# Pairwise products of 32 fields: VectorE keeps the order of the text

## The chip, the cores and the metric

The kernel runs on one core of a Trainium2 chip. The metric is the device time of one execution in microseconds (us), lower is better. The cited time is the median of three runs.

## The reference

The input is `r_x`, 4096 samples of 32 fields of 64 numbers each, and a 64 x 64 matrix `W`, all in 32-bit floats. Every field is multiplied by `W`, and then every pair of fields i < j gives one product, element by element:

```python
vid = jnp.einsum('bfd,de->bfe', x, W)
idx_i, idx_j = jnp.triu_indices(F_, k=1)      # F_ = 32: 496 pairs
return x[:, idx_i, :] * vid[:, idx_j, :]      # 4096 x 496 x 64
```

The input has 33.6 MB and the output 520 MB.

## The kernel before, in words

**Layout.** The host turns the samples so that the 64 numbers of a field lie across 64 partitions; two halves of the batch fill the 128 partitions. 128 samples of each half make one tile: 16 tiles, each 32 fields wide. One field (or one product) of a tile is a *unit* of 128 elements per partition. In SBUF there is one large buffer, `mem`, of 445 units, which holds everything: input tiles at the units in `XPLACE`, and products.

**Per tile** (loop of line 165), TensorE computes `vid` = x W for the 32 fields into PSUM, in eight blocks of four fields (two matmuls each, line 172). Then VectorE multiplies (line 196): one operand from `mem` (fields i), one from `vid` (fields j), the product into `mem`. `by_block` lists a tile's 496 pairs in blocks, and `products` cuts the blocks into instructions of 128 to 14336 elements per partition, 345 in all. Their order in the text is the order in which the products lie in the output.

**Slots.** The whole row of 16 x 496 products is cut into 70 runs, `SLOTS` (numbered from 0 here). Each names its length in units, the unit of `mem` where it is put, and the places ("seams") at which instructions are cut. When a slot's last product is written, line 199 issues one store of the whole slot to HBM. Slots overlap in `mem`: a later product writes where an earlier slot lay, and must wait until the parts that it overwrites have been stored. There are no pools that rotate; the list alone decides which store a product waits for. The slots that matter below:

| slot | units of `mem` | made by |
|---|---|---|
| 44, 45, 46 | 176 to 296, 297 to 413, 160 to 252 | tile 10 |
| 60 | 333 to 445 | tile 13 |
| 61 | 158 to 285 | tile 13 |
| 62 | 285 to 412 | end of tile 13, tile 14 |
| 63 | 64 to 191 | tile 14 |
| 64 | 192 to 319 | tile 14 |

Slots 65 to 69 follow to the end of tile 15.

**Order.** All transfers, loads and stores, are issued on the sync engine's queue (SP), in the order of the text. The kernel asks for that by name in line 121. For an engine that isn't named there, the framework's planner puts its instructions in an order of its own: it estimates when each can start and may let one pass others, as long as dependencies hold. Waits on semaphores are put in afterwards, for the order that results. VectorE isn't named in the kernel before, so its products may pass each other. Two of the 345 do:

- In tile 10, the 512-wide product of slot 46 (fields 0 to 3 with j = 24) stands ahead of four products that the text has before it: 8192 (the end of slot 44), 14336 and 512 (slot 45) and 1536 (the start of slot 46).
- In tile 14, the 10240-wide product of slot 63 (fields 0 to 15 with j = 16 to 20) stands ahead of five: 2048, 2048, 7168 and 768 (the end of slot 62) and 256 (the start of slot 63).

Of the kernel before, what the change touches and what calls it, by code (L numbers as in the profile page):

```python
# [52 lines left out]
def by_block():  # L53


    def within(lo):
        yield "step", lo, 2, 1, 0
        for k in range(2):
            yield "step", lo, 4, 2, k
        for i in (lo, lo + 8):  # L60
            yield "row", i + 4, i, 4, 4
        yield "row", lo + 8, lo, 8, 8

    yield from within(0)
    yield "row", 16, 0, 16, 16
    yield from within(16)


def products(blocks, at=0):

    for kind, a, b, c, d in blocks:
        if kind == "row":
            rows, n, i0, di, j0, dj = c, d, b, 0, a, 1
        else:
            rows, n, i0, di, j0, dj = 16 // b, c, a, b, a + c + d, b
        r = k = 0
        while r < rows:
            room = BREAKS[bisect_right(BREAKS, at)] - at
            if k or room < n:
                m, w = 1, min(n - k, room)  # L80
            else:
                m, w = min(rows - r, room // n), n
            yield at, m, w, i0 + r * di + k, di, j0 + r * dj, dj
            at += m * w
            if k + w == n:
                r, k = r + m, 0
            else:
                k += w
# [10 lines left out]
@with_exitstack  # L99
def pairwise_bilinear_kernel(  # L100
    ctx: ExitStack,
    tc: tile.TileContext,
    x0: bass.AP,
    x: bass.AP,
    out: bass.AP,
):

    nc = tc.nc
    NT = sum(len(tiles) for group in GROUPS for tiles in group)
    F = x0.shape[1] - 1 - PAD0
    D = P // 2
    NP = F * (F - 1) // 2

    BANK = 512 // C


    ctx.enter_context(tc.manual_schedule(engines={mybir.EngineType.SP}))

    const = ctx.enter_context(tc.tile_pool(name="const", bufs=1))
    psum = ctx.enter_context(
        tc.tile_pool(name="ps", bufs=1, space=bass.MemoryType.PSUM)
    )
    vid = psum.tile([P, F, C], F32)

    mem = const.tile([P, UNITS, C], F32)


    w2 = const.tile([P, D], F32)


    place = XPLACE[0]
    nc.sync.dma_start(  # L136
        out=mem.rearrange("p u c -> p (u c)")[:, place * C - D : (place + F // 2) * C],
        in_=x0.rearrange("p u c -> p (u c)")[:, C - D : (1 + F // 2) * C],
    )
    nc.sync.dma_start(out=mem[:, place + F // 2 : place + F, :], in_=x0[:, 1 + F // 2 : 1 + F, :])  # L140
    nc.vector.tensor_copy(w2, mem[:, place - 1, C - D :])  # L141
    loaded = 1

    def load(tiles, cuts=()):
        nonlocal loaded
        n = len(tiles) * F
        place = XPLACE[tiles[0]]
        at = (loaded - 1) * F
        loaded += len(tiles)
        return [  # L150
            nc.sync.dma_start(out=mem[:, place + lo : place + hi, :], in_=x[:, at + lo : at + hi, :])  # L151
            for lo, hi in cuts or [(0, n)]
        ]

    ready = mybir.DependencyInfo(mybir.DependencyClass.Sync, mybir.DependencyReason.DATA)

    def behind(later, earlier):
        tc.add_manual_dep(later.ins, earlier.ins.name, ready, reason="issued when that has landed")

    pieces = []  # L160
    groups, cuts = iter(GROUPS), iter(CUTS)
    for tiles, parts in zip(next(groups)[1:], next(cuts)):
        pieces = load(tiles, parts)

    for t in range(NT):
        xt = mem[:, XPLACE[t] : XPLACE[t] + F, :]


        for b in range(0, F, BANK):
            for h in range(2):  # L170
                half = slice(h * D, (h + 1) * D)
                nc.tensor.matmul(  # L172
                    vid[half, b : b + BANK, :],
                    lhsT=w2[half, :],
                    rhs=xt[half, b : b + BANK, :],
                    start=True,
                    stop=True,
                )

        for at, m, w, i, di, j, dj in products(by_block(), t * NP):  # L180
            slot = bisect_right(STARTS, at) - 1
            n = m * w
            begin, end = STARTS[slot], STARTS[slot + 1]
            ot = mem[:, SLOTS[slot][1] : SLOTS[slot][1] + SLOTS[slot][0], :]
            o = ot[:, at - begin : at - begin + n, :]
            if m == 1:
                left = xt[:, i : i + w, :]
                right = vid[:, j : j + 1, :].to_broadcast([P, w, C])
            else:
                o = o.rearrange("p (m w) c -> p m w c", m=m)  # L190
                right = vid[:, j : j + (m - 1) * dj + 1 : dj, :].unsqueeze(2).to_broadcast([P, m, w, C])
                if di == 0:
                    left = xt[:, i : i + w, :].unsqueeze(1).to_broadcast([P, m, w, C])
                else:
                    left = xt.rearrange("p (m d) c -> p m d c", d=di)[:, i // di : i // di + m, i % di : i % di + w, :]
            nc.vector.tensor_tensor(o, left, right, ALU.mult)  # L196
            at += n
            if at == end:
                store = nc.sync.dma_start(out=out[:, begin:end, :], in_=ot)  # L199
                if pieces:  # L200
                    behind(store, pieces[-2])
                    pieces.clear()


        if t + 2 == loaded < NT:
            (tiles,) = next(groups)
            pieces = load(tiles, next(cuts))
# [45 lines left out]
```

## Time and profile before

| | |
|---|---|
| time, median of 3 runs | 1291.11 us (1290.90 to 1291.38) |
| time of the profiled execution | 1290.48 us |
| span of the profiled execution, first to last instruction | 1288.7 us |
| VectorE busy (DVE) | 1084.0 us, 84% of the span, 346 instructions |
| TensorE busy (PE) | 219.6 us, 17%, 512 matmuls |
| transfers | 553.78 MB, 430 GB/s over the span |
| share of the 16 DMA engines taken by queue q1 | 99.6% |

The page has busy shares of the whole span and of 40 equal slices (32.2 us each), in tenths. "Idle before" in a row of a group is the time in which the engine had nothing running ahead of that instruction, with what ended it: `<-DMA out_dram<-mem` is the landing of an output transfer. A transfer is given from its issue to its landing, so it includes the time it waits behind others in the queue. The chain of waits goes back from the last instruction to what released it at each step.

### The profile page before, as it was taken

The page shows a single profiled execution, that of the slowest core. Times are in us where ns is not written, and L with a number is a line of the kernel's source. Part 1 is how long each engine was busy: PE and PEld are TensorE (multiplying, and loading weights), DVE is VectorE, ACT ScalarE, POOL GpSimd, SP SyncE. Part 2 cuts the span into 40 slices and gives each one's busy share as a digit, 9 for nine tenths or more (in the row PEclk, how much of TensorE's full clock was granted, in tenths as well). Part 3 has the DMA queues.
Part 4 walks back from the last instruction along what each step waited for, and adds up shares of the span by engine and source line. Part 5 has one row for each costly group of instructions (what it writes and reads, how often), then busy time and mean ns, then how long its engine had stood idle before and what let it go on. Part 6 is the DMA issues. An engine that isn't in the chain of part 4 may idle for free.

```text
span 1288.7 us, 1651 instructions
## 1 busy us (share of the span) xinstructions
PE 219.6 (17%) x512; PEld 42.2 (3%) x512; DVE 1084.0 (84%) x346; POOL 0.2 (0%) x4
## 2 busy tenths in 40 slices
PE   4031221203120213040312111103031130312000
PEld 1000000000000000000000000000000000000000
DVE  6899988899967389899799992859999889999942
POOL 0000000000000000000000000000000000000000
PEclk8555555656555556565555655555555565555555
DMA  9999999999999999999999999999999999989999
GB/s 416 432 423 439 443 436 423 434 424 443 420 453 411 422 435 431 443 439 430 423 442 427 433 443 430 423 418 432 447 433 418 441 440 418 448 361 452 435 414 412
DMA packets 11672, 553.78 MB, mean 430 GB/s; under 512 B 1296, under 2 KB 1296, under 8 KB 1680
## 3 DMA queue, kind: packets, MB, share of 16 engines
q1 hardware_dynamic: 11664, 553.69, 99.6%
q8 instruction: 4, 0.07, 0.0%
q14 instruction: 4, 0.03, 0.0%
HBM read 33.59 MB, written 520.09 MB: 430 GB/s over the span
## 4 chain that ended last, share of the span: by engine, by line
DMA 50%; DVE 42%; issue 6%; DVEq 0%; SPq 0%
DMA out_dram<-mem 45%; DVE mem L196 42%; DMA mem<-in_r_x_dram 5%; DVEq L241 0%; SPq L151 0%; DVEq L196 0%; SPq L140 0%; SPq L136 0%; SPq L199 0%
## 5 line engine op out<-in xcount | busy, mean ns | idle before, releaser
L196 DVE TENSOR_TENSOR mem<-mem,vid 128x1024 f32<-128x1024 f32 (+16 forms) x345 | 1083.8, 3213 | 173.6 <-DMA out_dram<-mem 168.1
L172 PE MATMUL vid<-mem,w 64*64 64x512 f32 x512 | 219.6, 988 | 961.1 <-DVE mem L196 853.3
L172 PEld LDWEIGHTS vid<-mem,w 64*64 64x64 f32 x512 | 42.2, 198 | 1137.3 <-DVE mem L196 984.8
L141 DVE COPY w<-mem 128x64 f32<-128x64 f32 x1 | 0.2, 195 | 5.8 <-DMA mem<-in_r_x_dram 5.8
L221 POOL MEMSET const-bfloat16-1.0<- 128x1 bf16 x1 | 0.1, 102 | 0.0
L221 POOL MEMSET const-uint8-127<- 128x1 uint8 x1 | 0.1, 102 | 0.0
L221 POOL MEMSET const-float32-0.0<- 128x1 f32 x1 | 0.1, 98 | 0.2 <-issue 0.2
L221 POOL MEMSET const-float32-1.0<- 128x1 f32 x1 | 0.1, 98 | 0.0
## 6 DMA issues: line engine op xcount, KB each, us to landing
out_dram<-mem SPq DMA_DIRECT2D x15, 8128.0 KB, 28.3
out_dram<-mem SPq DMA_DIRECT2D x14, 7680.0 KB, 24.6
out_dram<-mem SPq DMA_DIRECT2D x6, 7168.0 KB, 26.2
out_dram<-mem SPq DMA_DIRECT2D x5, 7936.0 KB, 28.1
out_dram<-mem SPq DMA_DIRECT2D x3, 7424.0 KB, 22.6
out_dram<-mem SPq DMA_DIRECT2D x3, 5888.0 KB, 20.9
mem<-in_r_x_dram SPq DMA_DIRECT2D x2, 8128.0 KB, 38.7
out_dram<-mem SPq DMA_DIRECT2D x2, 8064.0 KB, 24.4
```

The lines of the kernel that those rows point to most:

```text
L141: nc.vector.tensor_copy(w2, mem[:, place - 1, C - D :])
L172: nc.tensor.matmul(vid[half, b : b + BANK, :], lhsT=w2[half, :], rhs=xt[half, b : b + BANK, :], start=True, stop=True,)
L196: nc.vector.tensor_tensor(o, left, right, ALU.mult)
L221: nc = _bacc.Bacc("TRN2", target_bir_lowering=False, num_devices=1, dynamic_dma_scratch_size=1024)
```

## The change

VectorE is named beside the sync engine in the call that keeps the order of the text. Nothing else is edited.

```diff
-    ctx.enter_context(tc.manual_schedule(engines={mybir.EngineType.SP}))
+    ctx.enter_context(tc.manual_schedule(engines={mybir.EngineType.SP, mybir.EngineType.DVE}))
```

The built programs differ in this way: the two products above stand at their places in the text, and semaphore counts and waits follow that. In tile 14 the wait for slot 60's store, which the first 2048-wide product of slot 62's end had behind the 10240-wide one, now stands ahead of that product with nothing between. The instructions of TensorE, SP and GpSimd have the order they had.

## The prediction

> **What bounds the kernel now.** First the page's rows by 40 slices and its table of queues: they tell which resource is full, and where it isn't.
>
> ```profile
> DVE  6899988899967389899799992859999889999942
> ...
> DMA  9999999999999999999999999999999999989999
> GB/s 416 432 423 439 443 436 423 434 424 443 420 453 411 422 435 431 443 439 430 423 442 427 433 443 430 423 418 432 447 433 418 441 440 418 448 361 452 435 414 412
> ...
> q1 hardware_dynamic: 11664, 553.69, 99.6%
> ```
>
> The one hardware queue keeps the 16 DMA engines busy for 99.6% of the span, while VectorE (DVE) has slices at 2 and 3 tenths. The transfers are the bound. One slice alone shows an 8 in the DMA row and 361 GB/s: the 36th, 1128 to 1160 us. The table of stretches counts packets by their start and fixes the place:
>
> ```profile
> 1128.00:1131.00 3.00, 0.00 (x0) 0.00 (x0) 3.00 (x1) 0.00 (x0) 0.50 0.80 347
> 1131.30:1135.80 4.50, 1.65 (x4) 0.47 (x6) 4.50 (x4) 0.00 (x0) 0.50 0.00 0
> 1136.00:1139.00 3.00, 1.82 (x6) 0.14 (x2) 3.00 (x3) 0.00 (x0) 0.50 0.80 347
> ```
>
> The last two columns are DMA share and GB/s (with packets of 2.1 us counted by their start, 0.80 is what a full 3 us stretch shows here). From 1131.3 to 1135.8 us no packet starts at all, while VectorE is busy for the whole 4.50 us. It is the only such stretch: the queue has run dry. The chain of waits says what it waited for:
>
> ```profile
> 1061.31 0.06 DVE mem L196
> ...
> 1096.97 11.13 DVE mem L196 x6
> 1108.10 0.99 issue
> 1109.09 25.89 DVE mem L196 x8
> 1134.98 20.59 DMA out_dram<-mem
> ```
>
> The transfer issued at 1134.98 is slot 62's store. Ahead of it stand 73.7 us of products from 1061.31, with no wait between. The groups of VectorE between 1111.5 and 1134.9 us, shapes kept apart, show what ran last (busy us, mean ns, idle before):
>
> ```profile
> L196 DVE TENSOR_TENSOR mem<-mem,vid 128x10240 f32<-128x10240 f32 x1 | 10.8, 10809 | 0.0
> L196 DVE TENSOR_TENSOR mem<-mem,vid 128x7168 f32<-128x7168 f32 x1 | 7.6, 7611 | 0.0
> L196 DVE TENSOR_TENSOR mem<-mem,vid 128x2048 f32<-128x2048 f32 x2 | 4.5, 2276 | 0.0
> L196 DVE TENSOR_TENSOR mem<-mem,vid 128x768 f32<-128x768 f32 x1 | 0.9, 943 | 0.0
> ```
>
> The 10240-wide product belongs to slot 63; the four others finish slot 62. The planner put the former first.
>
> **What the Trainium skill says.** "Perfetto Trace Analysis", Optimization Strategy: look for gaps on the engine that bounds, and for what ends them; here that is the one hole above. "DMA: Bandwidth & Descriptors", Where 436 GB/s comes from, puts the ceiling of the SBUF ports at 435 GB/s, and about 358 for traffic with HBM; this trace runs at 430 with HBM, so it agrees with the first and not the second, and there is no rate left to gain. The same page, Why a DMA increments its semaphore by 16: each engine posts its own share when its data are down, so a transfer has landed with its slowest engine. The trace agrees: slot 61's store posted from 1132.02 to 1134.04 us. "Runtime: NRT & Kernel Launch", Instruction fetch mechanics: instructions are refilled in 16 KiB blocks by DMA, "mostly hidden". The trace has four such blocks; the last, at 1113.1 us, took 0.88 us of one DMA engine, which then stood about 2 us behind the others. That is not hidden where DMA is the bound.
>
> **The change part by part.** Instructions, slots, transfers and the order of SP and PE stay; the two built programs differ in the place of two products and in semaphore counts.
>
> Tile 10. A 512-wide product of slot 46 (0.68 us at 798.6) goes back behind the 8192, 14336, 512 and 1536 that the planner had let it pass. Where it leaves, VectorE waits anyway until 809.40 for a landing (10.14 us idle). Where it arrives, 835.3, the next product waits until 852.99, after 17.64 us of idle time. It is covered by 17 us, and the stores of slots 44 and 45 do not depend on it: 0 us. Without that cover it would be 0.68.
>
> Tile 14. The 10240 goes back behind two 2048s, 7168 and 768 of slot 62 and 256 of slot 63. That adds a wait: the first 2048 overlaps slot 60 by one unit (333), so slot 60's store must have landed. Its row is the sole issue near 1089.29 us:
>
> ```profile
> out_dram<-mem SPq DMA_DIRECT2D x1, 7168.0 KB, 25.9
> ```
>
> It lands at 1089.29 + 25.9 = 1115.2. Until now the 10.81 us product hid that; now VectorE stands from 1111.36 to 1115.2, **3.9 us of idle time**, with the four products and slot 62's store queued behind it. From the start of the first 2048 (1122.09) to the issue (1134.98) took 12.9 us, so the store goes out at 1115.2 + 12.9 = **1128.1 instead of 1135.0**. Its first packet followed the issue by 0.85 us: 1129.0. The earliest DMA engine falls idle at 1131.7. The hole closes, with 2.7 us to spare, although VectorE loses time.
>
> What is late next: VectorE's 3.9 us. The whole group, 10240 included, is done 3.9 us later, so slot 63's store goes from 1141.57 to 1145.4; the queue, then full of slot 62's 8128 KB (19.2 us, by the landings at 1155.57, 1174.81 and 1194.08), needs it at about 1131.7 + 19.2 = 1150.9. Slot 64: a wait of 1.46 us for slot 62's landing vanishes, 1160.44 + 3.9 - 1.5 = 1162.9 against 1170. Slots 65 to 68 shift by +2.4 us and less (other waits on landings vanish too) against spare times of 9 us and more. The last store, slot 69's, waits for slot 67's landing (1250.23 before, some 2.7 earlier after) and goes out near 1260.7 against a queue that is dry at 1264 at the earliest. No new hole.
>
> What the closed hole is worth. The slowest DMA engine landed slot 61's store at 1134.04; without a hole it would land slot 62's 19.24 later, 1153.28, instead of 1155.57: **2.29 us**. The mean engine was idle 3.8 us (each engine's gap in the packet records, 2.25 to 4.28). The hole also let all engines start level again (posts within 0.2 us of each other from there to the end); now the laggard keeps its lag. How much of it? After an earlier block, at 151.8, a lag of 2.14 (posts of the landing at 165.3) was 1.57 at 316.9, 152 us later, as long as what is left here. So I take 0.5 us back: 2.29 + 0.5 = **2.8 us**, with 2.3 (no recovery) and 3.8 (full) as ends. Which engine the block at 1113 meets is not mine to know: five of the 16 already lagged by 0.5 to 0.9 (posts of slot 61), and if it meets one of these, the gain is that much less, 1.9 to 2.3, and without recovery 1.4.
>
> Sum: 0 - 2.8. The profiled execution's own time, 1290.48 (span 1288.7 and 1.8 around it), becomes 1287.7. It stood 0.6 under the median of 1291.11, so the forecast for the median is 1288.4, -0.21%.
>
> **The rivals.** 0.2%, 2.6 us, is about what a measurement of this kernel can tell from no change.
>
> A. The hole closes, but a lagging engine eats most of it (the block meets a late engine, or no recovery): gain 1.4 to 2.5, 1288.6 to 1289.7, within 0.2%. For it: the lag of 2 us in the trace. Against: eleven engines of sixteen were level before the block, and earlier lags shrank.
>
> B. Nothing changes: the new wait takes the old one's place. That needs a landing of slot 60 near 1122, so that slot 62's store goes out near 1135 again; 1291.1. Against: the landing is set by a queue that is full, and the queue's end moves with it.
>
> C. Slower: the wait on slot 60's landing costs VectorE more than the passed-over 10240 did. It decides from a landing at 1122.1 on (1134.98 - 12.9), 6.9 us later than the trace's; each further us is one of DMA. A landing at 1125 gives 1294.0. For it: VectorE has no reserve of finished slots there, being the chain from 1061 on. Against: 18.9 us of queue lie between slot 60's landing and slot 61's, and only 13.7 between it and slot 62's first packet.
>
> D. The order of the text isn't what is built: excluded by the built programs, SP's order included.
>
> **How the numbers follow.** Main case with gain above 2.6 (up to 3.8): 0.51. A, and the main case under 2.6: 0.40, with B's 0.03 inside 0.2%: 0.43. C: 0.06. The likeliest time is 1288.4. From the full recovery (1287.3) to the late engine (1289.7) lie some 8 in 10; runs differ by 0.25 either way, and part of B is taken in at the top: 1287.0 to 1290.4.
>
> **What would show it.** In the changed profile: no stretch without packets around 1131 to 1136 and no slice at 361 GB/s; a VectorE wait of about 3.9 us for an output transfer ending near 1115.2; stores issued near 1128.1 and 1145.4; idle times before slots 64, 66 and 67 gone or shorter; the last landing spread over 1 us or more instead of 0.2. It is wrong if a new dry stretch appears behind slot 63, or if the 2048 starts after 1122, or if the span stays over 1287.5 with the hole gone (then the lag was mis-sized).

## The result, and the profile after

| | before | changed |
|---|---|---|
| time, median of 13 runs | 1291.01 us (1290.40 to 1291.38) | 1288.00 us (1287.81 to 1288.50) |
| ratio | | 0.9978, 95% interval 0.9970 to 0.9986 |
| profiled execution: time, span | 1290.48, 1288.7 us | 1287.95, 1286.2 us |
| share of the DMA engines taken by q1 | 99.6% | 99.8% |

The changed kernel is faster by 3.0 us, 0.22%. The rows of the page that showed the hole:

```profile
DVE  6899988899967389899799992849999889899952
...
DMA  9999999999999999999999999999999999999998
GB/s 415 417 440 440 440 416 447 420 442 425 435 432 437 421 424 430 434 440 431 424 443 423 435 444 438 417 426 436 438 430 422 443 437 425 441 429 423 436 444 383
...
q1 hardware_dynamic: 11664, 553.69, 99.8%
```

The 36th slice, 361 GB/s before, has 429. The only low slice is the last, and that one merely ends with the work. The same three stretches as before:

```profile
1128.00:1131.00 3.00, 2.68 (x8) 0.42 (x4) 3.00 (x3) 0.00 (x0) 0.63 0.95 412
1131.30:1135.80 4.50, 0.00 (x0) 0.00 (x0) 4.50 (x1) 0.00 (x0) 0.76 1.07 462
1136.00:1139.00 3.00, 0.00 (x0) 0.00 (x0) 3.00 (x1) 0.00 (x0) 0.50 0.85 368
```

In the middle one the share has gone from 0.00 to 1.07 (full, with packets counted by their start). VectorE is as busy as it was; it does the 10240-wide product there. The chain of waits up to that place:

```profile
1061.77 0.06 DVE mem L196
1061.83 12.81 issue
1074.64 15.09 DVE mem L196
1089.73 0.02 issue
1089.74 25.45 DMA out_dram<-mem
1115.20 0.03 issue
1115.23 0.02 DVEq L196
1115.25 0.04 issue
1115.29 0.20 DVE mem L196
```

A transfer now stands in a stretch that was products alone: slot 60's store, issued at 1089.74 and landed at 1115.20, releases the first 2048-wide product. VectorE's groups from there to slot 62's store, with the idle time before them in the last column:

```profile
L196 DVE TENSOR_TENSOR mem<-mem,vid 128x7168 f32<-128x7168 f32 x1 | 7.6, 7615 | 0.0
L196 DVE TENSOR_TENSOR mem<-mem,vid 128x2048 f32<-128x2048 f32 x2 | 4.5, 2284 | 3.4 <-DMA out_dram<-mem 3.4
L196 DVE TENSOR_TENSOR mem<-mem,vid 128x768 f32<-128x768 f32 x1 | 0.9, 947 | 0.0
```

The wait is 3.4 us long and new. The 10240-wide product no longer stands among them, and slot 62's store goes out at 1128.20 instead of 1134.98; its issue in the sync queue:

```profile
1128.20 0.33 SPq L199 DMA_DIRECT2D out_dram<-mem  x1
```

Over the whole span, VectorE's waits for output transfers are no longer than before (168.1 us in 37 waits then), though one was added:

```profile
DVE mem L196 <- DMA out_dram<-mem: 165.2, 34, 21.1
```

Four short waits behind that place (1.46, 0.20, 1.41 and 1.53 us before, between 1155 and 1231 us) are gone; from 1128.42 to 1234.28 us VectorE now runs 33 products with no wait between.

### The profile page after: what moved, and what is told of

The parts are those of the page before. It is cut to its first block, busy times and chain, and to the rows that moved or that the text cites. A ratio compares the mean times of both kernels' runs of the same rounds, so it can differ in the third digit from the quotient of the medians.

```text
span 1286.2 us, 1653 instructions
## 1 busy us (share of the span) xinstructions
PE 216.8 (17%) x512; PEld 41.5 (3%) x512; DVE 1083.7 (84%) x346; POOL 0.2 (0%) x4
## 3 DMA queue, kind: packets, MB, share of 16 engines
q1 hardware_dynamic: 11664, 553.69, 99.8%
## 4 chain that ended last, share of the span: by engine, by line
DMA 48%; DVE 44%; issue 6%; DVEq 0%; SPq 0%
DVE mem L196 44%; DMA out_dram<-mem 42%; DMA mem<-in_r_x_dram 5%; DVEq L241 0%; SPq L151 0%; DVEq L196 0%; SPq L140 0%; SPq L136 0%; SPq L199 0%
## 5 line engine op out<-in xcount | busy, mean ns | idle before, releaser
L196 DVE TENSOR_TENSOR mem<-mem,vid 128x1024 f32<-128x1024 f32 (+17 forms) x345 | 1083.5, 3213 | 171.2 <-DMA out_dram<-mem 165.2
L172 PE MATMUL vid<-mem,w 64*64 64x512 f32 x512 | 216.8, 975 | 966.8 <-DVE mem L196 858.8
```

The source lines that it names most:

```text
L172: nc.tensor.matmul(vid[half, b : b + BANK, :], lhsT=w2[half, :], rhs=xt[half, b : b + BANK, :], start=True, stop=True,)
```

## The experiments

**Theory.** The span is set by the DMA queue. The tile 14 move closes the queue's only hole, and that is the whole gain; its size is set by the slowest of the 16 DMA engines, which a 16 KiB block of instructions had put about 2 us behind. **Rivals:** the tile 10 move has a share; VectorE's work or wait is itself on the path; a hole costs the mean idle time of the engines; the lag has another cause.

All times below are medians, with the ratio to the kernel before on the same chip. Each of the 16 DMA engines posts to the semaphore of a transfer when its share is done. The *spread* of a landing is the time from the first of the 16 posts to the last, and an engine's *lag* is how far its post is behind the first. Posts and single packets stand in the traces' records, and in none of the views shown here.

| variant | time, us | ratio (95% interval) | slot 62's store issued at |
|---|---|---|---|
| kernel before (three chip sessions) | 1291.00, 1290.84, 1290.95 | | 1134.98 |
| tile 10 move alone | 1290.88 | 0.9999 (0.9991 to 1.0007) | 1135.52 |
| tile 14 move alone | 1288.09 | 0.9977 (0.9969 to 0.9986) | 1128.44 |
| slot 62 later by two products | 1288.81 | 0.9982 (0.9976 to 0.9989) | 1133.18 |
| slot 62 later by four | 1293.50 | 1.0019 (1.0012 to 1.0027) | 1138.13 |
| wait partly filled | 1287.99 | 0.9978 (0.9969 to 0.9986) | 1128.98 |
| short TensorE stream | 1286.98, again 1287.24 | 0.9972 (0.9961 to 0.9983), 0.9970 (0.9959 to 0.9982) | 1127.37, 1127.20 |
| the same with a late block | 1288.12 | 0.9977 (0.9969 to 0.9986) | 1128.34 |
| changed kernel again | 1288.04 | 0.9976 (0.9966 to 0.9985) | 1126.71 |

**1. Which of the two moves.** Each variant takes the text's order and puts one product back by hand to where the planner had it. First, the tile 10 move alone:

```diff
+        work = list(products(by_block(), t * NP))
+        if t == 14:
+            work.insert(3, work.pop(8))
+        for at, m, w, i, di, j, dj in work:
-        for at, m, w, i, di, j, dj in products(by_block(), t * NP):
```

> Text order everywhere but in tile 14, where the 10240-wide product is put ahead of slot 62's four last products by hand: only the tile 10 move is left. Theory (the hole before slot 62's store is the whole gain): time as before, 1291.0 within 0.4; slot 62's store issued near 1135 us; a stretch without packets from about 1131.5 to 1135.8. Rival (VectorE is the bound, and each product that passes others costs something): part of the 3.0 us remains, 1288.5 to 1290.

Measured: 1290.88, as the kernel before. The hole is back; the stretch table has

```profile
1131.30:1135.80 4.50, 1.12 (x4) 0.29 (x4) 4.50 (x4) 0.00 (x0) 0.50 0.04 14
```

a DMA share of 0.04. The tile 10 move is worth nothing. The counterpart is the same edit with `t == 10` and `work.insert(5, work.pop(9))`:

> Text order everywhere but in tile 10, where the 512-wide product of slot 46 passes four others as before: only the tile 14 move is left. Theory: the same as the changed kernel, 1288.0 within 0.4; slot 62's store issued near 1128.2. Rival (the tile 10 move has a share): 1288.7 to 1290.

Measured: 1288.09, the whole gain, with the stretch full:

```profile
1131.30:1135.80 4.50, 0.00 (x0) 0.00 (x0) 4.50 (x1) 0.00 (x0) 0.88 1.07 462
```

**2. How much a hole costs.** The changed kernel with slot 62's store made later by repeats of one of its products, here two:

```diff
-            nc.vector.tensor_tensor(o, left, right, ALU.mult)
+            for _ in range(3 if (t, m, w, i, j) == (14, 4, 4, 8, 12) else 1):
+                nc.vector.tensor_tensor(o, left, right, ALU.mult)
```

> The changed kernel with the second 2048-wide product of slot 62's end made three times instead of once (same values): VectorE gets 2 x 2.2 = 4.4 us more work, slot 62's store goes out at about 1132.6, its first packet starts at 1133.5. Theory (the end is set by the slowest DMA engine, which falls idle only at about 1133.9): most engines stand idle for 1 to 1.5 us and nothing is lost, 1288.0 to 1288.3, and the last landing's spread falls from 1.45 to 0.3 to 0.8. Rival (a hole costs its mean length over the engines): +1.0 to 1.3, 1289.0 to 1289.3. Rival (VectorE's work is the path): +4.4, 1292.4.

Measured: 1288.81, 0.8 above the changed kernel (spans 1286.9 and 1286.2). The store's issue in the sync queue, and a stretch of the hole:

```profile
1133.18 0.33 SPq L199 DMA_DIRECT2D out_dram<-mem  x1
```

```profile
1132.40:1133.90 1.50, 1.50 (x4) 0.42 (x6) 1.50 (x3) 0.00 (x0) 0.50 0.00 0
```

No packet of data starts for 1.5 us, and yet most of the gain stays. All three expectations were missed, the theory's too (its time, and a last spread of 0.3 to 0.8, where 0.22 was measured). The store was 0.6 us later than I had reckoned: a repeat takes 2.32 us rather than 2.2 (from the wait's end to the issue it is 12.91 us without repeats and 17.55 with two), and the wait ended 0.34 later. And I had left out my own term for recovery. The slowest engine landed slot 61's store at 1134.41; all 16 then landed slot 62's within 0.16 us of each other, at the latest at 1153.78, so it lost 0.1 us to the hole itself (19.37 instead of 19.24). From slot 61's last landing to that of the last store it took 151.65 us, in the changed kernel 150.98. Of the 0.7 us between, 0.5 is the lag that the slowest engine made up in the changed kernel and that is not there to make up here: the engines, once level, stay level (spreads of 0.16 to 0.23 to the end). The mean engine stood idle for 1.6 us (its posts for slot 62, 1153.68 in the mean, less 19.24 and less those for slot 61, 1132.85). So the mean-idle rival, at the measured issue, would have given 1289.6 and VectorE's work as the path 1292.6; the slowest engine's account, added up after the run, gives 1288.6 to 1288.7. The interval of the ratio reaches up to 0.9989 of 1291.0, which is 1289.6, so the median alone does not quite exclude the mean-idle rival. But none of the 19 runs took more than 1289.23, and the trace shows it directly: the mean engine lost 1.6 us in this hole and the slowest 0.1.

> The same product made five times: +8.8 us of VectorE work, slot 62's store at about 1137.0, first packet at 1137.85, 2.0 later than in the kernel before. Theory: all engines have run dry, start level and end 2.0 after those of the kernel before: 1293.0, and the last landing's spread is 0.2; 4.4 us more than the variant with three, though it has the same added work beyond it as that one has beyond the changed kernel. Rival (mean idle of the engines): 1288.0 + 5.6 = 1293.6. Rival (VectorE's work is the path): 1288.0 + 8.8 = 1296.8.

With five instead of three in that line, the time was 1293.50. The store goes out at 1138.13, and the engines have all run dry, the slowest included:

```profile
1132.60:1138.90 6.30, 1.61 (x4) 0.47 (x6) 6.30 (x4) 0.00 (x0) 0.50 0.00 0
```

The last landing's spread is 0.20, as expected for a level start. The first two repeats cost 0.8 us, the next two 4.7: little while the slowest engine still works, and nearly microsecond for microsecond after that (the store 4.95 us later, the span 4.96 longer). Against the kernel before, the store is 3.15 later, but 0.69 of that was there already at the landing that starts VectorE's long stretch (1061.91 against 1061.22). The other 2.46 is the 2.5 by which the medians differ. The theory's 1293.0 was 0.5 too low, as the four repeats took 2.32 us each here too, and not 2.2. The time does not tell the theory from the mean-idle rival, which had expected 1293.6; the variant with two does.

**3. Whether VectorE's new wait costs anything.** The changed kernel with two short products of slot 63 moved into the wait: the tile 14 edit of experiment 1 with `work[3:3] = [work.pop(9), work.pop(7)]`.

> The changed kernel with two short products of slot 63 (1536 and 256 wide, 2.0 us together) ahead of slot 62's first 2048, so that they fill part of VectorE's new wait of 3.4 us. Theory (that wait is covered by the queue): no change against the changed kernel, 1288.0 within 0.4, the wait for the landing shorter by 2.0, slot 62's store still at 1128.2 and slot 63's about 2.0 earlier, at 1143.5. Rival (the new wait is on the path that sets the end): 2.0 less, 1286.0.

Measured: 1287.99. The wait before the first 2048 is the bracket of this row of the timeline:

```profile
1116.07 12.02 DVE L196 TENSOR_TENSOR mem<-mem,vid 128x2048 f32<-128x2048 f32 x3 [1.73 <-DMA out_dram<-mem]
```

It fell from 3.41 to 1.73, and the time did not move: that wait is covered. Slot 63's store went out at 1144.31, 1.2 earlier than in the changed kernel; this execution's landing of slot 60 was 0.8 later, which makes up the expected 2.0.

**4. Where the lag comes from.** The changed kernel with half the matmuls, so that TensorE's stream of instructions crosses its last 16 KiB boundary far from the end. `w2` is 128 x 128 with W in two diagonal blocks and zeros elsewhere; the lines that fill it, and the smaller reserve of scratch memory, are left out here, and each matmul call stands on one line:

```diff
-            for h in range(2):
-                half = slice(h * D, (h + 1) * D)
-                nc.tensor.matmul(vid[half, b : b + BANK, :], lhsT=w2[half, :], rhs=xt[half, b : b + BANK, :], start=True, stop=True)
+            nc.tensor.matmul(vid[:, b : b + BANK, :], lhsT=w2, rhs=xt[:, b : b + BANK, :], start=True, stop=True)
+        for _ in range(36 if t == 1 else 0):
+            nc.tensor.matmul(vid[:, F - 1, :8], lhsT=w2, rhs=xt[:, F - 1, :8], start=True, stop=True)
```

> The changed kernel with one 128-row matmul by a block-diagonal copy of W in place of two 64-row ones, and 36 tiny matmuls in tile 1 that write again what is there, so that TensorE's instruction stream crosses its last 16 KiB boundary near tile 9 instead of tile 14 (the reserve of scratch memory for DMA is halved to make room for the larger W). Theory (the laggard DMA engine of the last 170 us is made by the fetch of the block near 1103 us): no such packet after about 800 us, the landing of slot 60's store has a spread near 1.0 instead of 2.0, the last landing 0.6 to 0.9 instead of 1.45, and the time is 0.4 to 0.8 less than that of the changed kernel, 1287.2 to 1287.6. Rival (the lag has another cause): spread 2.0 at slot 60, 1288.0.

Measured: 1286.98, the fastest median of all, 0.2 under the expected range; the repeat below, 1287.24, lies in it. The page's row for instruction blocks is

```profile
q8 instruction: 2, 0.03, 0.0%
```

two blocks instead of four, by the packet records at 103.1 and 643.6 us. The landings of slots 60 and 61 have spreads of 1.01 and 0.91 (2.01 and 1.94 in the changed kernel) and the last 0.54 (1.45).

That variant differs in its matmuls too. So the control has the same matmuls and only 54 tiny ones in place of 36 (the page counts each twice, x108 and x72), which brings a third block, late; the other two kernels ran beside it on one chip.

> The variant with the block-diagonal W again, with 54 tiny matmuls in tile 1 instead of 36, so that TensorE's stream is longer by 36 matmuls and crosses one more 16 KiB boundary, near tile 14, at 1050 to 1150 us; nothing else differs. Theory (the late block makes the laggard): a 16 KiB packet there, a spread of the landings of about 2.0 just after it, 1.3 to 1.5 at the last landing, time as the changed kernel, 0.6 to 1.0 above the variant with 36. Rival (the gain of that variant came from the shorter or other matmuls): time as the variant with 36.

> The variant with 36 tiny matmuls once more, beside the other two on one chip: 0.6 to 1.0 less than the changed kernel, by the same reason (last landing's spread 0.6 instead of 1.45).

> The changed kernel itself beside them on the same chip: 1288.0, 0.9978 of the kernel before.

Measured: 1288.12 with the late block, 1287.24 without, 1288.04 for the changed kernel. The control's page has

```profile
q8 instruction: 3, 0.05, 0.0%
```

and the third lies at 1113.3 us. The spread of its landings is 1.02 at slot 59, before the block, 2.39 at slot 60, just after it, and 1.63 at the last (2.0, and 1.3 to 1.5, were expected); without the block slot 60 has 0.97 and the last 0.65. The intervals of the ratios overlap, so the 0.9 us between the medians is not settled by the times alone. That the late block makes the laggard is. The second block comes at 480.4 us in one execution and at 643.8 in the other, but their spreads at slots 56 to 59 agree within 0.02; then one has the block. At the last landing the control's mean engine is 0.26 us earlier than without the late block (1283.84 and 1284.10), and its slowest engine is 0.70 later (1285.25 and 1284.55).

## Why the prediction was right

It said 1288.4 us (1287.0 to 1290.4), 0.21% faster; measured 1288.0, 0.22%. Faster by over 0.2% had been given 0.51 and within 0.2% had 0.43, and the interval of the ratio lies on both sides of that bound. The mechanism held step by step; that the median fell on the favoured side of 0.2% was partly luck, as the two spans differ by 2.5 us, just under it.

| step | predicted | changed profile |
|---|---|---|
| dry stretch near 1131 to 1136 | gone | gone |
| VectorE's new wait | 3.9 us, to 1115.2 | 3.41 us, to 1115.3 |
| slot 62's store | 1128.1 | 1128.20 |
| slots 63, 64 | 1145.4, 1162.9 | 1145.52, 1162.84 |
| last store | 1260.7 | 1260.96 |
| spread of the last landing | 1 or more | 1.45 |
| slot 61's last landing to the end's | shorter by 2.8 | 153.81 to 150.98, by 2.83 |

- **The tile 10 move** at 0 us: right, shown by experiment 1.
- **The wait** came out 0.5 shorter because in this execution VectorE reached it 0.5 later, at 1111.88; the landing, which ends it, hardly moved. It was covered, as reckoned (experiment 3).
- **The size of the hole** was the step that decided between the main case and rival A, and it held: 2.29 for the slowest engine and 0.5 of recovery. Measured: slot 62's last landing follows slot 61's by 19.15 us instead of 21.53, which is 2.38, and the spread fell from 1.94 at slot 61 to 1.45 at the end.
- **The total** reads 2.5 in the two spans and 3.0 in the medians. The profiled execution after was 0.45 late at 1061 us, well ahead of the change's place, and 0.30 late at slot 61's last landing; 2.83 less 0.30 is 2.5. The rest is within what runs of one kernel differ by (0.7 us among the 13 here, up to 2.0 in the later sessions).
- **Rival A's fear**, that the block would meet an engine that was late already, did not come true in this trace. Five engines were more than 0.4 us behind at slot 59 (0.55 to 1.06) and six at slot 60, five with nearly the same lags and a new one with 2.01: the block met a level engine. It came at 1102.9 rather than 1113.1, which changed little (the spread at slot 61 is 1.94; 2.02 before).
- **Rivals B and C** needed slot 60's landing at 1122 or later; it was at 1115.20. The variant with four repeats shows what C would have looked like: the store 3.15 us later than before, and 1293.5.
- **Two readings** in it are too wide, with no effect on the sum. In the dry stretch no packet of data starts, but 16 packets of 4 bytes do, one ahead of each engine's post for slot 61. And 0.80 is not the fixed mark of a full stretch of 3 us: by packet starts, the full stretches in these tables show 0.80 to 0.95.

## What to carry to other kernels

Where transfers bound a kernel, look for the stretch in which no packet of data starts, and ask what the one engine that feeds the queue did just before it: here, moving a long product out from in front of the last pieces of a store paid, although it gave that engine a new wait. The holes here cost what they cost the slowest of the 16 engines, so size a hole by the last landing and not by the mean share. What the planner took the landing times to be is not on record; compare its order with the text's wherever the bound resource has run dry.

## What the runs showed of the hardware

A block of instructions is one packet of 16 KiB, which took 0.88 to 1.00 us, but it puts the DMA engine that fetches it behind by about 2 us. The packet records of the changed kernel show where the rest goes: the packet of data that ends where the late block starts took 2.69 us instead of 2.12 and the one that starts where it ends 2.53 instead of 2.12, so that with the block's 0.88 this engine lost 1.86 us. Why those two are slower, the runs do not show. The spread of the landings grew by less, by 0.95 in the changed kernel and 1.37 in the control, because other engines lagged already.

Where the queue is full, such a lag stays: the changed kernel's last spread, 1.45, is only 0.5 us smaller than slot 61's, 151 us before it. The Trainium skill ("Runtime: NRT & Kernel Launch", Instruction fetch mechanics) calls the cost of such a block "mostly hidden". For TensorE this trace agrees, since its next matmuls after the late block, at 1106.22 us, were released by a product; for a full DMA queue it does not. The five executions with a late block and no later hole ended with a spread of 1.43 to 1.72, the two without a late block with 0.54 and 0.65. Since the number of TensorE instructions decides when the block comes, fewer matmuls went with a faster kernel, though TensorE is busy for only 17% of the changed kernel's span (19% of the faster one's).

One execution looks different: in the repeated run of the changed kernel the spread was 1.83 before the late block, and 2.05 after it. There too six engines instead of five lagged once the block had come, but the five were late by 1.3 to 1.8 already. Blocks are not the only source of lag: in every run the spread rises from at most 0.87 at the store that landed near 406 us to between 1.23 and 2.15 at the load that landed near 427 us, with no block between. What put five engines so far behind in this execution, the runs do not show. Its profiled run took 1286.72 us, 1.3 less than its kernel's median, in spite of the largest last spread; 0.8 us of that was there at slot 57's landing near 1061 us, ahead of the change's place, so that most of its low time comes from elsewhere.
